# Layer 0's output in two passes over the chunks, and layer 1 placed ahead of the branch on the flag

## The chip, the cores and the metric

The kernel runs on one core of a Trainium2 chip. The metric is the device time of one execution in microseconds (us). Three runs of the kernel before took 7120.3, 7141.34 and 7145.82 us (median 7141.34). One further execution was recorded by the hardware profiler; it took 7152.27 us, of which 7150.5 us lie between its first and its last instruction (its span). All positions below, such as "at 6925.4", are us from the start of that span.

The engines are TensorE (PE; its weight loads are PEld), VectorE (DVE), ScalarE (ACT), GpSimd (POOL) and SyncE (SP). A row of SP or POOL with "q" is the issue of a DMA, not its transfer.

## The reference

Two layers work on 2708 nodes of 128 features, with a sparse adjacency matrix `adj` of 2708 x 2708. Layer 0 is a graph attention with 8 heads' worth of channels, layer 1 two graph convolutions. Each is followed by a residual sum and a normalisation over the features.

```python
# layer 0
q = (x @ Wq.T).reshape(d, n, h); k = ...; v = ...
a = einsum('dnh,dmh->dnm', q, k) * d ** -0.5 + adj + adj
out = einsum('dnm,dmh->dnh', softmax(a, axis=2), v)
x = layernorm(x + out.reshape(n, h * d) @ Wo.T)
# layer 1
local_hidden = adj @ (x @ W2) + b2
local_cross = adj @ (local_hidden @ W4) + b4
x = layernorm(x + local_cross + local_hidden @ res_w.T + res_b)
```

## The kernel before, in words

The kernel works in four stages. Everything is float32.

1. **Projections** (up to about 250 us): q, k and v are computed and written to HBM.
2. **Attention** (up to 6765): for 32 groups of 4 channels and 6 blocks of query nodes, scores, exponentials and their products with v. It leaves its sums in HBM as `os`: 8 rows of numerators and one row of denominators, for each channel and node. Its last result is copied out of PSUM at 6764.4 (line 377) and stored by four DMAs (line 379).
3. **Layer 0's output** (`layer0_out`, lines 479 to 516, up to 6915.8): the 2708 rows are worked on as 22 chunks (`MC`: 21 of 128 rows, one of 20). Each chunk goes through one long chain:
   - SP loads `ot` (128 x 9 x 128, 576 KB, in pieces of 512 bytes, line 484) and `xt` (64 KB, line 486).
   - DVE takes the reciprocal of the denominators (`rd`, line 488) and multiplies (`on`, line 490).
   - PE transposes `on` in 8 pieces into PSUM (`pt`, line 493), ACT copies that to SBUF (`oT`, line 495), and PE multiplies by Wo in 8 products (`py`, line 498; a float32 product is two matmul records in the profile).
   - DVE adds the residual (`y`, line 500) and takes the statistics (`st`, `mv`, lines 470 and 472), ACT takes the root (`sd`, 474), DVE inverts it (`rs`, 476) and normalises (`x1`, 477).
   - PE transposes `x1` (`px`, 511), ACT copies it (`x1T`, 513), PE multiplies by W2 (`pw`, 515), ACT copies the result (`xw`, 516).

   In the same loop DVE judges the result (`judge`): whether each denominator lies between two limits (`ok`, lines 503 to 505) and whether `y` is finite (lines 507 and 508), five instructions for each chunk. At the end the verdicts are brought down to one number, `n_fine` (lines 526 to 536).
4. **The branch and layer 1.** All engines load `n_fine` into a register (line 537) and branch (line 539). Where the verdict is bad, a slower attention (`attention_with_maxima`) and `layer0_out` are done again; with these inputs they are jumped over. Then layer 1 runs: for each of its two products, over 6 blocks of columns (`NBS`: 5 of 512, one of 148), `propagate` loads 22 tiles of `adjT` (256 KB each, `col`, issued by POOL at line 558, into 24 buffers) and PE multiplies each by the chunk of `xw` or `hw` that belongs to it, all into one accumulator (`acc`, line 559). After a block of the first product PE also multiplies by W4 (`ph`, 570); after a block of the second, by the residual weights (line 562), and the block's 4 row chunks are normalised and stored (line 584, issued by SP).

What sets the order: each engine works through its own instructions in order, and so do the DMA queues of SP and POOL: a DMA that waits holds all those behind it. Outside the attention, a scheduler chose that order when the program was built. In the order that it made, the chain of chunk c + 1 on PE stands behind that of chunk c at several places: `px` and `pw` of a chunk come ahead of the `py` of the next.

Pools set how far loads run ahead: three buffers for `ot` and `xt`, two for the accumulators in PSUM, 24 for `col`.

Of the kernel before, what the change touches and what calls it, by code (L numbers as in the profile page):

```python
# [9 lines left out]
F32 = mybir.dt.float32  # L10
F32R = mybir.dt.float32r
I32 = mybir.dt.int32
AF = mybir.ActivationFunctionType
ALU = mybir.AluOpType
AX = mybir.AxisListType
PSUM = bass.MemoryType.PSUM
DRAM = bass.MemoryType.DRAM

P = 128
H = 8  # L20
GB = 4
NB = 512
# [4 lines left out]
SUM_LOW = 1e-6  # L27
SUM_HIGH = 1e30


QK_LIMIT = 7.5
# [3 lines left out]
def chunks(n, w):  # L35
    return [(i, min(w, n - i)) for i in range(0, n, w)]
# [93 lines left out]
def graph_attention_gcn(ctx: ExitStack, tc: tile.TileContext, x, xT, adj, adjT, adjP, adjS,  # L130
# [325 lines left out]
        nc.sync.dma_start(t, src)  # L456
    nc.vector.tensor_add(bias, b4_sb, rb_sb)

    x1 = keep.tile([P, NM, D], F32, name="x1")
    xw = keep.tile([P, NM, D], F32, name="xw")  # L460
    hw = keep.tile([P, NM, D], F32, name="hw")
    lhT = keep.tile([P, N], F32, name="lhT")
    eps = keep.tile([P, 1], F32, name="eps")
    nc.vector.memset(eps, EPS)
    fine = keep.tile([P, NM + 1, 4], F32, name="fine")
    nc.vector.memset(fine, 1.0)

    def layernorm(to, y, w):
        st = stat.tile([P, nc.vector.BN_STATS_DIM], F32, tag="st", name="st")
        nc.vector.bn_stats(st[:w], y)  # L470
        mv = stat.tile([P, nc.vector.BN_AGGR_DIM], F32, tag="mv", name="mv")
        nc.vector.bn_aggr(mv[:w], st[:w])  # L472
        sd = stat.tile([P, 1], F32, tag="sd", name="sd")
        nc.scalar.activation(sd[:w], mv[:w, 1:2], AF.Sqrt, bias=eps[:w])  # L474
        rs = stat.tile([P, 1], F32, tag="rs", name="rs")
        nc.vector.reciprocal(rs[:w], sd[:w])  # L476
        nc.vector.tensor_scalar(to, y, mv[:w, 0:1], rs[:w], ALU.subtract, ALU.mult)  # L477

    def layer0_out(sb, ps, pa, judge):

        o3 = os_.rearrange("e (i g) -> i e g", g=P)
        for c, (i0, w) in enumerate(MC):
            ot = sb.tile([P, H + 1, P], F32, tag="ot", name="ot")
            nc.sync.dma_start(ot[:w], o3[ds(i0, w)])
            xt = sb.tile([P, D], F32, tag="xt", name="xt")
            nc.sync.dma_start(xt[:w], x[ds(i0, w), :])
            rd = sb.tile([P, P], F32, tag="rd", name="rd")
            nc.vector.reciprocal(rd[:w], ot[:w, H, :])
            on = sb.tile([P, H, P], F32, tag="on", name="on")
            nc.vector.tensor_mul(on[:w], ot[:w, :H, :], rd[:w].unsqueeze(1).to_broadcast([w, H, P]))  # L490
            pt = ps.tile([P, H, P], F32, tag="wide", name="pt")
            for e in range(H):
                nc.tensor.transpose(pt[:, e, :w], on[:w, e, :], ident[:w, :w])
            oT = sb.tile([P, H, P], F32, tag="oT", name="oT")
            nc.scalar.copy(oT[:, :, :w], pt[:, :, :w])
            py = pa.tile([P, NB], F32, tag="narrow", name="py")
            for e in range(H):
                nc.tensor.matmul(py[:w, :D], oT[:, e, :w], wo[:, e, :], start=(e == 0), stop=(e == H - 1))
            y = sb.tile([P, D], F32, tag="y", name="y")
            nc.vector.tensor_add(y[:w], py[:w, :D], xt[:w])  # L500
            if judge:
                ok = sb.tile([P, P], F32, tag="ok", name="ok")
                nc.vector.tensor_scalar(ok[:w], ot[:w, H, :], SUM_LOW, None, ALU.is_ge)
                nc.vector.scalar_tensor_tensor(ok[:w], ot[:w, H, :], SUM_HIGH, ok[:w], ALU.is_le, ALU.mult)
                nc.vector.tensor_reduce(fine[:w, c, 0:1], ok[:w], AX.X, ALU.min)
                finite = sb.tile([P, P], F32, tag="finite", name="finite")
                nc.vector.tensor_scalar(finite[:w], y[:w], 0.0, 0.0, ALU.mult, ALU.is_equal)
                nc.vector.tensor_reduce(fine[:w, c, 1:2], finite[:w], AX.X, ALU.min)
            layernorm(x1[:w, c, :], y[:w], w)
            px = pa.tile([P, NB], F32, tag="narrow", name="px")  # L510
            nc.tensor.transpose(px[:, :w], x1[:w, c, :], ident[:w, :w])
            x1T = sb.tile([P, P], F32, tag="x1T", name="x1T")
            nc.scalar.copy(x1T[:, :w], px[:, :w])
            pw = pa.tile([P, NB], F32, tag="narrow", name="pw")
            nc.tensor.matmul(pw[:w, :D], x1T[:, :w], w2, start=True, stop=True)
            nc.scalar.copy(xw[:w, c, :], pw[:w, :D])

    with ExitStack() as s:
        sb = s.enter_context(tc.tile_pool(name="sb1", bufs=3))
        ps = s.enter_context(tc.tile_pool(name="ps1", bufs=2, space=PSUM))  # L520
        pa = s.enter_context(tc.tile_pool(name="psa", bufs=2, space=PSUM))
        layer0_out(sb, ps, pa, True)
        for i in range(2):
            for j, (way, op) in enumerate(((ALU.max, ALU.is_le), (ALU.min, ALU.is_ge))):
                end = keep.tile([P, 1], F32, name=f"end{i}{j}")
                nc.vector.tensor_reduce(end, ends[:, i, j, :], AX.X, way)
                limit = QK_LIMIT * (1.0, half_scale)[i] * (1 if j == 0 else -1)
                nc.vector.tensor_scalar(fine[:, NM, 2 * i + j : 2 * i + j + 1], end, limit, None, op)
        every = keep.tile([P, 1], F32, name="every")
        nc.vector.tensor_reduce(every, fine.rearrange("p c t -> p (c t)"), AX.X, ALU.min)  # L530
        ones = keep.tile([P, 1], F32, name="ones")
        nc.vector.memset(ones, 1.0)
        pf = pa.tile([P, NB], F32, tag="narrow", name="pf")
        nc.tensor.matmul(pf[:1, :1], every, ones, start=True, stop=True)
        n_fine = keep.tile([1, 1], I32, name="n_fine")
        nc.vector.tensor_copy(n_fine, pf[:1, :1])
    rows_fine = nc.values_load(n_fine, min_val=0, max_val=P)

    with tc.If(rows_fine < P), ExitStack() as s:  # L539
        with ExitStack() as t:  # L540
            attention_with_maxima(t, tc, qs, ks, vs, os_, adj, adjT, ident)
        sb = s.enter_context(tc.tile_pool(name="sb0", bufs=2))
        ps = s.enter_context(tc.tile_pool(name="ps0", bufs=2, space=PSUM))
        pa = s.enter_context(tc.tile_pool(name="pa0", bufs=2, space=PSUM))
        layer0_out(sb, ps, pa, False)


    sb = ctx.enter_context(tc.tile_pool(name="sb2", bufs=3))
    cols = ctx.enter_context(tc.tile_pool(name="cols1", bufs=24))
    ps = ctx.enter_context(tc.tile_pool(name="ps2", bufs=2, space=PSUM))  # L550
    pa = ctx.enter_context(tc.tile_pool(name="pa2", bufs=2, space=PSUM))

    def propagate(src, n0, nw, last=None):

        acc = ps.tile([P, NB], F32, tag="wide", name="acc1")
        for m, (m0, mw) in enumerate(MC):
            t = cols.tile([P, NB], F32, tag="col", name="col1")
            nc.gpsimd.dma_start(t[:mw, :nw], adjT[ds(m0, mw), ds(n0, nw)])  # L558
            nc.tensor.matmul(acc[:, :nw], src[:mw, m, :], t[:mw, :nw], start=(m == 0),  # L559
                             stop=(last is None and m == NM - 1))  # L560
        if last is not None:
            nc.tensor.matmul(acc[:, :nw], *last, start=False, stop=True)  # L562
        return acc

    for n0, nw in NBS:
        acc = propagate(xw, n0, nw)
        nc.vector.tensor_scalar(lhT[:, ds(n0, nw)], acc[:, :nw], b2_sb, None, ALU.add)
        for i, w in chunks(nw, P):
            ph = pa.tile([P, NB], F32, tag="narrow", name="ph")
            nc.tensor.matmul(ph[:w, :D], lhT[:, ds(n0 + i, w)], w4, start=True, stop=True)  # L570
            nc.scalar.copy(hw[:w, (n0 + i) // P, :], ph[:w, :D])  # L571

    for n0, nw in NBS:
        acc = propagate(hw, n0, nw, (rw, lhT[:, ds(n0, nw)]))
        eT = sb.tile([P, NB], F32, tag="eT", name="eT")
        nc.vector.tensor_scalar(eT[:, :nw], acc[:, :nw], bias, None, ALU.add)  # L576
        for i, w in chunks(nw, P):
            pe = pa.tile([P, NB], F32, tag="narrow", name="pe")
            nc.tensor.transpose(pe[:w, :D], eT[:, ds(i, w)], ident)  # L579
            y = sb.tile([P, D], F32, tag="y", name="y1")  # L580
            nc.vector.tensor_add(y[:w], pe[:w, :D], x1[:w, (n0 + i) // P, :])  # L581
            o = sb.tile([P, D], F32, tag="xo", name="xo")
            layernorm(o[:w], y[:w], w)
            nc.sync.dma_start(out[ds(n0 + i, w), :], o[:w])


def attention_with_maxima(ctx, tc, qs, ks, vs, os_, adj, adjT, ident):
# [124 lines left out]
```

## Time and profile before

| | |
|---|---|
| runs | 7120.3, 7141.34, 7145.82 us |
| profiled execution, its span | 7152.27 us, 7150.5 us |
| PE, DVE, ACT, POOL busy in the span | 6813.9, 6156.5, 6560.1, 5755.0 us |
| attention's last copy ends | 6765.0 |
| layer 0's output: first reciprocal to the flag | 6767.5 to 6915.8 |
| branch, first load of layer 1 and first product | 6916.4, 6921.9, 6925.4 |
| layer 1: first product to the last normalised row | 6925.4 to 7148.0 |
| layer 0's output, one chunk: `rd`, `on` on DVE | 0.95, 1.21 us |
| `pt` (8 transposes) at full and half clock | 1.09, 1.97 us |
| `oT` on ACT | 1.01 us |
| `py` (16 records) at full and half clock | 1.95, 3.62 us |
| `y`, `st`, `mv` on DVE | 0.29, 0.28, 0.17 us |
| copy of 128 columns on ACT (`x1T`, `xw`) | 0.27 us |
| load of ACT's function table | 1.28 us |
| layer 1: one product, 128 x 512 (two records), full clock | 0.86 us |

How to read it: the busy shares of the page are averages over 7150 us, of which the attention is more than nine tenths, so they say nothing of the stages that the change touches. These are read by windows of time and by the timeline, whose rows give the start and the length of a group of instructions, the engine, the line, the operation, and in brackets how long the engine stood idle before it and what ended that. "PEclk" is the TensorE clock that was granted, as a share of full speed.

### The profile page before, as it was taken

What the parts mean: (1) busy time and instruction counts of PE and PEld (TensorE: products, weight loads), DVE (VectorE), ACT (ScalarE), POOL (GpSimd) and SP (SyncE); (2) the same over time, 40 slices, a digit from 0 to 9 for tenths busy, and PEclk for the clock granted to TensorE, in tenths of its full rate; (3) what the DMA queues carried; (4) which work ended last, traced back from release to release, by engine and by line L of the source; (5) the groups of instructions that cost most, each with busy time, mean ns of one, the idle gap of its engine ahead of it and who ended that gap; (6) DMA issues with size and microseconds to landing.
All of it is one profiled execution on the core that took longest, in us unless ns stands there. A gap on an engine that the chain in (4) does not pass through costs nothing. (4 is left out here: it accounts for less than half of the span.)

```text
span 7150.5 us, 136834 instructions
## 1 busy us (share of the span) xinstructions
PE 6813.9 (95%) x50426; PEld 2184.1 (31%) x50426; DVE 6156.5 (86%) x6292; ACT 6560.1 (92%) x3710; POOL 5755.0 (80%) x2525
## 2 busy tenths in 40 slices
PE   6599999999999999999999999999999999999979
PEld 2122233223332332222222332332322232323354
DVE  7589899989998998898899998998989998989831
ACT  3699999999999999999999999999999999999810
POOL 0578888888888888888888888888888888888625
PEclk9799999999999999999999999999999999999979
DMA  9776767767766767776677677677667767766647
GB/s 288 223 245 231 231 224 242 234 221 241 232 226 228 244 222 226 235 239 220 219 239 232 224 242 235 221 237 232 223 222 242 234 222 232 245 222 222 202 151 238
DMA packets 1101142, 1642.67 MB, mean 230 GB/s; under 512 B 144516, under 2 KB 1078804, under 8 KB 1096236
## 3 DMA queue, kind: packets, MB, share of 16 engines
q1 hardware_dynamic: 1081260, 1575.13, 67.7%
q0 software_dynamic: 19200, 58.68, 2.4%
q8 instruction: 399, 6.54, 0.4%
q14 instruction: 283, 2.32, 0.1%
HBM read 1551.44 MB, written 81.80 MB: 228 GB/s over the span
## 5 line engine op out<-in xcount | busy, mean ns | idle before, releaser
L441 POOL TENSOR_TENSOR w<-w,ecol 128x1356 f32<-128x1356 f32 (+1 forms) x1728 | 5351.6, 3104 | 925.2 <-ACT w L440 837.6
L357 DVE TENSOR_TENSOR e<-s,col 128x904 f32<-128x904 f32 (+1 forms) x4608 | 4830.4, 1092 | 483.9 <-PE s L350 172.7
L443 ACT ACTIVATE e<-e 128x2712 f32<-128x2712 f32 (+5 forms) x1728 | 4707.8, 2724 | 2.7 <-DVE e L357 2.5
L371 PE MATMUL acc<-e,vals 128*32 128x452 f32 x21888 | 3839.4, 557 | 11.4 <-ACT e L443 0.6
L350 PE MATMUL s<-q,k 32*128 32x452 f32 x10944 | 2464.1, 468 | 191.3 <-DVE e L357 80.6
L440 ACT ACTIVATE w<-p 128x1356 f32<-128x1356 f32 (+1 forms) x1728 | 2396.3, 1387 | 72.2 <-PE p L350 64.4
L350 PEld LDWEIGHTS s<-q,k 32*128 32x128 f32 x10944 | 1025.7, 182 | 3358.0 <-DVE e L357 2833.3
L371 PE MATMUL acc<-w,vals 128*32 128x452 f32 x10368 | 1670.2, 558 | 0.0
L350 PE MATMUL p<-q,k 32*128 32x452 f32 (+1 forms) x5184 | 1272.7, 439 | 12.3 <-ACT w L440 12.1
L357 DVE TENSOR_TENSOR e<-s,two 128x904 f32<-128x904 f32 (+1 forms) x960 | 1048.2, 1092 | 191.0 <-ACT w L440 82.6
L371 PEld LDWEIGHTS acc<-e,vals 128*32 128x32 f32 x21888 | 621.2, 108 | 855.0 <-issue 787.5
L350 PEld LDWEIGHTS p<-q,k 32*128 32x128 f32 x5184 | 521.2, 183 | 30.7 <-ACT w L440 30.1
L371 PEld LDWEIGHTS acc<-w,vals 128*32 128x32 f32 x10368 | 280.2, 108 | 205.1 <-issue 179.6
L558 POOL DMA_DIRECT2D col<-in_adjT x264 | 141.3, 537 | 231.9 <-SPq L539 159.2
L291 POOL CAST k<-k_raw 128x336 fp32r<-128x336 f32 x256 | 226.3, 886 | 15.1 <-DMA v_short<-vs 15.1
L367 PE MATMUL acc<-e,v_short 128*128 128x452 f32 (+1 forms) x384 | 196.7, 594 | 0.0
L233 POOL MEMSET k_short<- 128x128 f32 x2 | 0.3, 205 | 203.4 <-DMA vs<-po 203.4
L205 ACT ACTIVATE pr<-pp 128x1024 fp32r<-128x1024 f32 (+1 forms) x44 | 45.0, 1024 | 112.4 <-DMA ks<-pr 52.5
L377 DVE COPY o<-acc 128x452 f32<-128x452 f32 x192 | 118.5, 617 | 6.2 <-PE acc L371 6.2
L474 ACT ACTIVATE sd<-mv,eps 128x1 f32<-128x1 f32 (+1 forms) x44 | 12.5, 293 | 120.5 <-DVE mv L472 118.4
L559 PE MATMUL acc<-col,xw 128*128 128x512 f32 (+2 forms) x264 | 106.3, 556 | 9.8 <-DMA col<-in_adjT 9.8
L571 ACT COPY hw<-ph 128x128 f32<-128x128 f32 (+1 forms) x22 | 5.4, 266 | 115.3 <-PE ph L570 115.3
(73 smaller groups left out, 1251.0 us busy)
## 6 DMA issues: line engine op xcount, KB each, us to landing
col<-in_adjP SPq DMA_DIRECT2D x1965, 226.0 KB
two<-in_adjP SPq DMA_DIRECT2D x1440, 226.0 KB
ecol<-ne SPq DMA_DIRECT2D x1395, 226.0 KB
col<-in_adjP SPq DMA_DIRECT2D x393, 224.0 KB
two<-in_adjP SPq DMA_DIRECT2D x288, 224.0 KB
ecol<-ne SPq DMA_DIRECT2D x279, 224.0 KB
col<-in_adjT POOLq DMA_DIRECT2D x210, 256.0 KB, 4.5
k_raw<-ks SPq DMA_DIRECT2D x512, 84.6 KB
```

Source lines behind the costliest of these rows:

```text
L205: nc.scalar.mul(o[:mi, 0], flat, f)
L291: nc.gpsimd.tensor_copy(k[:, :, ts(i, n)], t[:, ts(i, n * NU)].rearrange("p (q c) -> p c q", c=NU))
L350: nc.tensor.matmul(to[:, :nw], k[r, m, :], q[r, :nw], start=True, stop=True)
L357: nc.vector.tensor_add(e[:, ds(at, 2), :nw], st[:, :, :nw], a)
L367: nc.tensor.matmul(a[:, :nw], vz, e[:, t, :nw], start=False, stop=False)
L371: nc.tensor.matmul(a[ds(32 * j, VW), :nw], v[:, m, ds(VW * j, VW)], e[:, t, :nw], start=(m == first_chunk), stop=(m == last_chunk))
L377: nc.vector.tensor_copy(o[:, :nw], acc.pop((g, b))[:, :nw])
L440: nc.scalar.activation(w[:, :, :nw], sp[:, :, :nw], AF.Exp, scale=2.0)
L441: nc.gpsimd.tensor_mul(w[:, :, :nw], w[:, :, :nw], exp_cols[g, b, two][:, :nw].unsqueeze(1).to_broadcast([P, 3, nw]))
L443: nc.scalar.activation(e[:, :at, :nw], e[:, :at, :nw], AF.Exp, scale=2.0)
L558: nc.gpsimd.dma_start(t[:mw, :nw], adjT[ds(m0, mw), ds(n0, nw)])
L559: nc.tensor.matmul(acc[:, :nw], src[:mw, m, :], t[:mw, :nw], start=(m == 0), stop=(last is None and m == NM - 1))
```

## The change

`layer0_out` is rewritten as passes over all chunks. The first is a loop with a pipeline written out by hand: `load` two chunks ahead, `divide` (load to `oT`) for chunk c, `project` (`py`) for chunk c - 1, `add_x` (`y` and its statistics) for chunk c - 2. The sums `y` of all chunks are kept in a new array `ys`, their means and variances in `mvs`. Behind the loop stand one root and one reciprocal for all 22 chunks, and a second pass in groups of four chunks: normalise, transpose into one PSUM tile `px`, one copy, multiply by W2 into one tile `pw`, one copy. The judging keeps, for each chunk, only the smallest and the largest denominator (`reach`); whether `ys` is finite is asked once for the whole array, after the second pass.

The order of these instructions is the written one (`manual_schedule`), engine by engine; layer 1's are still placed by the scheduler, which may put them between.

Layer 1 becomes a function. It is called right behind `layer0_out`, ahead of the branch, and its pool of 24 `col` buffers is opened before `layer0_out`'s pools. Its `col` loads are issued by SP and no longer by POOL. The branch comes last; its body does the slower attention and then both layers again (`rest(False)`).

```diff
+    nc.gpsimd.memset(eps, EPS)
+    nc.gpsimd.memset(ys[:, NM - 1, :], 0.0)
+    mvs = keep.tile([P, NM, nc.vector.BN_AGGR_DIM], F32, name="mvs")
+    nc.gpsimd.memset(mvs, 1.0)
...
-        for c, (i0, w) in enumerate(MC):
+        def load(c):
+            i0, w = MC[c]
             ot = sb.tile([P, H + 1, P], F32, tag="ot", name="ot")
             nc.sync.dma_start(ot[:w], o3[ds(i0, w)])
             xt = sb.tile([P, D], F32, tag="xt", name="xt")
             nc.sync.dma_start(xt[:w], x[ds(i0, w), :])
+            given[c] = ot, xt
+
+        def divide(c):
+            w, ot = MC[c][1], given[c][0]
             rd = sb.tile([P, P], F32, tag="rd", name="rd")
             nc.vector.reciprocal(rd[:w], ot[:w, H, :])
+            if judge:
+                for i, op in enumerate((ALU.min, ALU.max)):
+                    nc.vector.tensor_reduce(reach[:w, i, c : c + 1], ot[:w, H, :], AX.X, op)
             on = sb.tile([P, H, P], F32, tag="on", name="on")
...
+        def project(c):
+            w, oT = MC[c][1], turned.pop(c)
+            made[c] = pa.tile([P, NB], F32, tag="py", name="py", bufs=2)
...
+        def add_x(c):
+            w = MC[c][1]
+            nc.vector.tensor_add(ys[:w, c, :], made.pop(c)[:w, :D], given.pop(c)[1][:w])
+            statistics(mvs[:w, c, :], ys[:w, c, :], w)
...
-                ok = sb.tile([P, P], F32, tag="ok", name="ok")
-                nc.vector.tensor_scalar(ok[:w], ot[:w, H, :], SUM_LOW, None, ALU.is_ge)
-                nc.vector.scalar_tensor_tensor(ok[:w], ot[:w, H, :], SUM_HIGH, ok[:w], ALU.is_le, ALU.mult)
-                nc.vector.tensor_reduce(fine[:w, c, 0:1], ok[:w], AX.X, ALU.min)
-                finite = sb.tile([P, P], F32, tag="finite", name="finite")
-                nc.vector.tensor_scalar(finite[:w], y[:w], 0.0, 0.0, ALU.mult, ALU.is_equal)
-                nc.vector.tensor_reduce(fine[:w, c, 1:2], finite[:w], AX.X, ALU.min)
-            layernorm(x1[:w, c, :], y[:w], w)
-            px = pa.tile([P, NB], F32, tag="narrow", name="px")
-            nc.tensor.transpose(px[:, :w], x1[:w, c, :], ident[:w, :w])
-            x1T = sb.tile([P, P], F32, tag="x1T", name="x1T")
-            nc.scalar.copy(x1T[:, :w], px[:, :w])
-            pw = pa.tile([P, NB], F32, tag="narrow", name="pw")
-            nc.tensor.matmul(pw[:w, :D], x1T[:, :w], w2, start=True, stop=True)
-            nc.scalar.copy(xw[:w, c, :], pw[:w, :D])
...
+        load(0)
+        load(1)
+        for c in range(NM + 2):
+            if c + 2 < NM:
+                load(c + 2)
+            if c < NM:
+                divide(c)
+            if 0 <= c - 1 < NM:
+                project(c - 1)
+            if c >= 2:
+                add_x(c - 2)
+        sd, rs = (sb.tile([P, NM], F32, tag=n, name=n) for n in ("sds", "rss"))
+        nc.scalar.activation(sd, mvs[:, :, 1], AF.Sqrt, bias=eps)
+        nc.vector.reciprocal(rs, sd)
+        for c0 in range(0, NM, 4):
...
+            for c in cs:
+                w = MC[c][1]
+                nc.vector.tensor_scalar(x1[:w, c, :], ys[:w, c, :], mvs[:w, c, 0:1], rs[:w, c : c + 1],
+                                        ALU.subtract, ALU.mult)
+                nc.tensor.transpose(px[:, c - c0, :w], x1[:w, c, :], ident[:w, :w])
+
+            full = len([c for c in cs if MC[c][1] == P])
+            parts = [(0, full, P)] + [(c - c0, 1, MC[c][1]) for c in cs if MC[c][1] < P]
+            for i, n, w in parts:
+                nc.scalar.copy(x1T[:, ds(i, n), :w], px[:, ds(i, n), :w])
+            for c in cs:
+                w = MC[c][1]
+                nc.tensor.matmul(pw[:w, c - c0, :], x1T[:, c - c0, :w], w2, start=True, stop=True)
+            for i, n, w in parts:
+                nc.scalar.copy(xw[:w, ds(c0 + i, n), :], pw[:w, ds(i, n), :])
+        if judge:
+            finite = sb.tile([P, NM * D], F32, tag="finite", name="finite", bufs=1)
+            nc.vector.tensor_scalar(finite, ys.rearrange("p c f -> p (c f)"), 0.0, 0.0, ALU.mult, ALU.is_equal)
+            nc.vector.tensor_reduce(fine[:, 0:1], finite, AX.X, ALU.min)
...
+            nc.tensor.matmul(pf[:1, :1], every, ones, start=True, stop=True)
+            nc.vector.tensor_copy(n_fine, pf[:1, :1])
...
-            nc.gpsimd.dma_start(t[:mw, :nw], adjT[ds(m0, mw), ds(n0, nw)])
+                nc.sync.dma_start(t[:mw, :nw], adjT[ds(m0, mw), ds(n0, nw)])
...
+    def rest(judge):
+        with ExitStack() as s:
+            cols = s.enter_context(tc.tile_pool(name="cols1", bufs=24))
+            with ExitStack() as t:
+                sb = t.enter_context(tc.tile_pool(name="sb1", bufs=3))
+                ps = t.enter_context(tc.tile_pool(name="ps1", bufs=2, space=PSUM))
+                pa = t.enter_context(tc.tile_pool(name="psa", bufs=1, space=PSUM))
+                t.enter_context(tc.manual_schedule())
+                layer0_out(sb, ps, pa, judge)
+            layer1(s, cols)
+
+    n_fine = keep.tile([1, 1], I32, name="n_fine")
+    rest(True)
     rows_fine = nc.values_load(n_fine, min_val=0, max_val=P)
-    with tc.If(rows_fine < P), ExitStack() as s:
+    with tc.If(rows_fine < P):
         with ExitStack() as t:
             attention_with_maxima(t, tc, qs, ks, vs, os_, adj, adjT, ident)
-        layer0_out(sb, ps, pa, False)
+        rest(False)
```

The order of the changed program's instructions, engine by engine, is known before it runs. On SP the four stores of `os` and the loads of the weights come first, then three pairs of `ot` and `xt`; from there a pair stands as "xt of chunk c, then ot of chunk c + 1", with one or two `col` loads behind it, until 24 `col` tiles are placed. `xt` of chunk c waits for `add_x` of chunk c - 3, because it takes over that chunk's buffer. Behind the 29th `col` load stands its load of `n_fine` into a register. On PE the products of layer 1's first block stand one by one between the groups of the second pass (five of them), and the product `pf` that sums the verdicts stands ahead of the sixth.

## The prediction

> **What bounds the kernel now.** The chain of waits that ended last lies wholly in layer 1 and is PE's (line 559), so ahead of 6921 it tells nothing. I read the tail by windows of time first; columns: length, busy time of PE, PEld, DVE, ACT, POOL with counts, granted clock, DMA share, GB/s.
>
> ```profile
> 6841.00:6878.00 37.00, 24.92 (x193) 21.93 (x191) 22.05 (x71) 13.87 (x30) 0.00 (x0) 1.00 0.13 38
> 6878.00:6913.00 35.00, 24.11 (x103) 19.99 (x103) 6.80 (x31) 5.43 (x17) 0.00 (x0) 0.51 0.02 5
> 6913.00:6926.00 13.00, 1.21 (x6) 0.92 (x7) 1.52 (x8) 0.73 (x3) 4.13 (x8) 0.63 0.24 69
> 6936.00:7140.00 204.00, 204.00 (x553) 94.07 (x552) 23.67 (x95) 9.64 (x38) 129.41 (x242) 1.00 0.82 271
> ```
>
> In layer 1 (last row) PE is never idle: it is the bound there. In layer 0's output (first two) no engine is full, DMA is idle: a chain of latencies. Around the branch (third) nothing works. The timeline shows the chain for one chunk at full clock, and for one of the last five at half clock:
>
> ```profile
> 6866.90 1.01 ACT L495 COPY oT<-pt 128x1024 f32<-128x1024 f32 x1 [1.58 <-PE py L498]
> 6867.96 1.09 PE L493 MATMUL pt<-ident,on 128*128 128x128 f32 x8 [1.16 <-ACT oT L495]
> 6869.90 1.95 PE L498 MATMUL py<-wo,oT 128*128 128x128 f32 x16
> 6871.94 1.01 ACT L495 COPY oT<-pt 128x1024 f32<-128x1024 f32 x1 [1.57 <-PE py L498]
> ...
> 6891.19 0.29 DVE L500 TENSOR_TENSOR y<-py,xt 128x128 f32<-128x128 f32 x1 [5.20 <-PE py L498]
> ```
>
> A chunk takes 5.04 us at full clock (6866.90 to 6871.94): ACT copies only once `py` is done, PE transposes only once ACT has copied. The last five take 7.1 each. The waits of SP, and two reciprocals with the loads they wait for:
>
> ```profile
> SPq L486 <- DVE finite L507: 80.6, 19, 7.0
> SPq L539 <- SPq L539: 4.1, 1, 4.1
> ```
>
> ```profile
> 6821.32 0.37 SPq L484 DMA_DIRECT2D ot<-os  x1
> ...
> 6825.12 4.03 SPq L484 DMA_DIRECT2D ot<-os  x2
> ...
> 6826.20 0.95 DVE L488 RECIPROCAL rd<-ot 128x128 f32<-128x128 f32 x1 [0.42 <-DMA ot<-os]
> ...
> 6829.62 0.95 DVE L488 RECIPROCAL rd<-ot 128x128 f32<-128x128 f32 x1 [0.34 <-DMA ot<-os]
> ```
>
> SP waits 80 us in all for DVE to free an `xt` (a wait for several at once; line 500 is the reader). The other pair: from the issue of an `ot` to its use pass 4.9 us (the 17th, 6821.32 to 6826.20) and 4.5 us (the 18th, 6825.12 to 6829.62). The branch takes 4.1 us.
>
> I call E the moment when PE starts the sixth product of layer 1, since the new order puts five of them into the second pass. Before: first product 6925.4; at half clock a record takes 0.86 us to about 6930.2, then 0.43: ten records end at **E = 6932.0**. Behind E the work is the same.
>
> **First pass.** Up to the first `ot` SP's list is nearly the old one (four stores, weights, biases); the old trace has its next load at 6771.28, where `ot` of chunk 0 now stands (two were loaded before the attention's end, so this start is later than now). Plus 4.7 us of landing: first reciprocal 6776.0, 8.5 us later than now. From first reciprocal to first `y` the trace has 9.95 us (6767.52 to 6777.47, half clock); two reductions of 0.25 come in between: **first `y` at 6786.4**.
>
> From then on each engine's share of a chunk is: PE 1.09 + 1.95 = 3.04; ACT 1.01; DVE 0.95 + 2 x 0.25 + 1.21 + 0.29 + 0.28 + 0.17 = 3.40 by durations, about 3.2 by starts, since instructions overlap by some 0.06 (`on` follows `rd` at 0.87). The new order takes ACT and PE off each other's back. What is late next is **SP**: `ot` of chunk c + 1 stands behind `xt` of chunk c, and that waits for `add_x` of c - 3. From the end of one `y`: `xt` and `ot` issue 0.4, landing 4.7, `rd` 0.87, two reductions 0.4, `on` 1.2, `y` 0.3 = 7.9 us to the `y` two chunks on, so **3.9 us a chunk**. The `col` loads share the DMAs: 24 tiles, 1 or 2 a chunk; at 369 GB/s (10 us window from 6926) one takes 0.7 us, and part of that stands ahead of an `ot`; I add 0.1 us over 13 chunks: 3.95 on average. The DMAs carry 640 + 384 KB a chunk: 2.8 us at that rate, 3.9 at the 267 GB/s of the best slice of layer 0's output, so they may just share the bound. 19 chunks x 3.95 = 75 us: 6861.4; the last two `y` come without loads, 0.5 + 2.5 + 0.67 + 0.3 + 1.95 + hops = 6.7: **last `y` at 6868.1**.
>
> The clock: here the Trainium skill speaks against the change. "TensorE: Matmul & The Clock Gate", Part 4, says that transposes do not count as work that raises the clock. Without them PE would be busy 1.95 / 3.95 = 49% of a chunk; in the first window (full clock) the products are (14.23 + 3.42) / 37 = 48%, in the second (half clock) (18.09 + 3.99) / 35 = 63%, doubled by the slow clock. So products alone don't tell the two windows apart, and I go by the first row: 67% busy with transposes held full clock for 37 us, and the new loop has 3.04 / 3.95 = 77%. By the rule PE could stay at half clock: 1.97 + 3.62 = 5.6 us a chunk, PE the bound, 19 x 1.65 = 31 us later.
>
> **Second pass.** Now 22 chains of `st` to `xw` stand in the loop; they become: statistics 0.45, the table load 1.28 (it stands behind the wait for the last `mv`, so it is paid here), root 0.29, reciprocal 0.16, first four `x1` about 1.2, `px` 0.5 to 0.9, hops: 5 us. Then six groups, each a copy 128 x 512 (0.59, between 0.27 for 128 columns and 1.01 for 1024), `pw` (8 records, 1.0 at full and 1.8 at half clock), another copy 0.59, hops 0.4: 2.6 us by ACT; by PE `px`, `pw` and one product of layer 1, 2.3 at full, 4.4 at half clock. I take 2.8 x 5.5 = 15.5: `pf` is due at 6888.6. DVE meanwhile: 22 `x1` (0.26 apart) to 6876, then `finite` over 2816 columns (0.225 for 128; by 1.0 to 1.4 ns a column from the 512-wide rows: 3 to 4), its reduction 3, twelve small ones 2.5: 6885 to 6887. Hidden, just. If it were 3 us late, PE would stand at `pf`. **E = 6888.6, 43.4 us earlier.** I give back 1 us for a window at half clock behind it.
>
> **Judging** in the loop falls from 1.25 to 0.5 us of DVE a chunk; worth nothing by itself, DVE was not the bound.
>
> **Layer 1.** PE stays the bound. `col` issues move from POOL (0.54 each) to SP (0.35 to 0.43), one per 0.86 us of PE: covered by 24 buffers. Behind SP's load of `n_fine` wait `col` loads from the 30th on, until about 6888; 24 tiles lie ready, 20 us of PE. Each `out` store now stands ahead of `col` loads; the worst waits some 9 us (from the 16th product of a block to its end and 3 us of normalising), with loads for 12 us in hand. Bounds: 0 to 3 us in all; I take 0. The memsets on POOL are hidden, POOL has been idle since 6762.7.
>
> **The end.** The branch's gap (n_fine at 6915.8 to the first product 6925.4) is in the 43.4. It comes back once behind the last store: 4.1 us of branch and 0.6 of semaphore resets, in place of the 1.1 us in which SP now awaits the store's landing: **+3.6**. If fetching the code ran ahead: +0; if both branches of the end miss: +7.7.
>
> **Sum:** -43.4 + 1 + 3.6 = **-38.8 us**. Against the profiled execution 7152.27: 7113.5. The runs' median is 11 us lower than that, and I take the difference from it: 7141.3 - 38.8 = **7102 us**. The attention's instructions and their order are unchanged.
>
> **Rivals.**
> - *DVE sets the loop*: `ot` lands earlier, as the three buffers suggest, 3.2 us a chunk: 19 x 0.75 = 14 us better, 7088. For: DVE's durations alone. Against: the order of `xt` and `ot` on SP. 20%.
> - *Half clock* through the loop, as worked out: 7133; partial windows, 7120. For: ahead of 6841 the clock flipped all the time. Against: a PE that is full at half clock was raised again (6838 to 6841). 16%.
> - *Slower*: `col` loads ahead of `ot` on SP's queue hold it up. Price: 0.5 us a chunk for each us of landing, 19 chunks. The gain of 39 is gone at 4.1 us more, 8.8 us of landing; at 10 us: 7102 + 19 x 2.65 = 7152. For: five `col` loads stand in one row behind the fourth `ot`. Against: only 1 or 2 a chunk follow, and DMA was 13% busy. 4%.
> - *It doesn't do what it says*: the scheduler could leave layer 1 behind the flag. The order shows the opposite; none.
>
> The likeliest, SP's loop, has the remaining 60%, by itself 7092 to 7114.
>
> **Numbers.** A measurement tells about 0.5% (36 us) from nothing: the line is at 7105.6. Of the likeliest case 70% lies below it: 42 + 20 = 62% faster, 18 + 16 = 34% the same, 4% slower. The range 7078 to 7128 leaves out the far ends of the first two rivals and the third.
>
> **What will show it.** `rd` about 3.9 us apart and waiting for `ot`; if for PE, half clock. Clock 1.0 from about 6790 on. `pf` near 6888. PE without idle time behind it. Some 4 us between the last store and the end. Wrong would be: `rd` at 3.2 or over 5 us apart, or PE waiting for `col`.

## The result and the profile after

The changed kernel takes 7108.9 us (median of 8 runs, 7088.4 to 7116.2) against 7145.8 us of the kernel before (8 runs): a ratio of 0.995, 95% interval 0.9934 to 0.9966, so between 24 and 47 us off. The profiled execution spans 7109.3 us where the one of before spans 7150.5. The attention is unchanged, but its end differs from one execution to the next (6765.0 us in the first, 6772.3 in the second), so from here on each stage is counted from the end of the attention's last copy, and **tail** is what comes behind that copy.

| us behind the attention's last copy | before | after |
|---|---|---|
| first reciprocal `rd` | 2.5 | 9.5 |
| first `y` added | 12.2 | 18.1 |
| last `y` added | 147.7 | 95.8 |
| sixth product of layer 1 (E) | 167.1 | 115.1 |
| last `xo` | 383.0 | 331.1 |
| end of the span | 385.5 | 337.0 |
| at half clock, up to the last `xo` | 81.9 | 21.4 |

The positions in the table are starts; that of the last `xo` is its end. First the windows of the changed kernel (columns as before): the loop, the start of the second pass, layer 1, and what follows the last `xo`.

```profile
6791.00:6863.00 72.00, 52.90 (x449) 50.00 (x448) 57.48 (x132) 19.23 (x19) 0.00 (x0) 1.00 0.75 223
6869.00:6877.00 8.00, 4.92 (x17) 3.76 (x18) 6.28 (x24) 3.35 (x5) 0.00 (x0) 0.59 0.00 1
6888.00:7091.00 203.00, 203.00 (x540) 92.83 (x538) 22.07 (x90) 9.68 (x38) 0.00 (x0) 1.00 0.81 260
7103.42:7109.30 5.88, 0.00 (x0) 0.00 (x0) 0.01 (x1) 0.00 (x0) 0.00 (x0) 0.50 0.09 24
```

The loop runs at full clock throughout, and still no engine is full in it: PE 73%, DVE 80%, the DMA engines 75%. Something else sets its pace. Layer 1 is PE's to the last microsecond, as it was. The last row is the new end: 5.9 us in which nothing computes. The timeline shows two chunks of the loop:

```profile
6817.60 0.28 DVE L521 TENSOR_TENSOR ys<-py,xt 128x128 f32<-128x128 f32 x1
...
6817.91 0.33 SPq L495 DMA_DIRECT2D xt<-in_x  x1
...
6818.28 0.43 SPq L493 DMA_DIRECT2D ot<-os  x1
...
6819.07 0.95 DVE L501 RECIPROCAL rd<-ot 128x128 f32<-128x128 f32 x1 [0.64 <-DMA ot<-os]
...
6823.03 0.95 DVE L501 RECIPROCAL rd<-ot 128x128 f32<-128x128 f32 x1 [0.80 <-DMA ot<-os]
...
6825.36 0.28 DVE L521 TENSOR_TENSOR ys<-py,xt 128x128 f32<-128x128 f32 x1
```

Read it as a circle. The addition into `ys` at 6817.60 frees an `xt`; only then SP issues the waiting `xt` load (6817.91) and behind it the `ot` load (6818.28); 4.75 us later the reciprocal that needs this `ot` starts (6823.03, DVE had idled for it), and its iteration ends with the next addition but one, 6825.36. That is 7.76 us for two chunks. The waits of SP say the same, and price the branch:

```profile
SPq L495 <- DVE st L473: 51.0, 19, 4.2
...
SPq L630 <- SPq L630: 2.9, 1, 2.9
```

All 19 `xt` loads that need a used buffer wait, 51 us together. (DVE's line is that of the instruction nearest to the event; the reader of `xt` is the addition just ahead of it.) The branch itself is 2.9 us at the end; before, it was 4.1 us in the middle. The second pass, in the timelines of ACT, DVE and PE:

```profile
6869.04 1.28 ACT L536 ACT_TABLE_LOAD   x1 [4.36 <-DVE mvs L474]
...
6883.04 0.16 DVE L571 TENSOR_REDUCE every<-fine 128x1 f32<-128x7 f32 x1
...
6887.32 0.19 PE L574 MATMUL pf<-ones,every 128*1 128x1 f32 x2
6887.45 7.99 PE L588 MATMUL acc<-col,xw 128*128 128x512 f32 x18
```

The table load stands on the path behind the last statistics. The flag's chain on DVE is done at 6883.2, and PE comes to `pf` only at 6887.3: the chain is hidden, with 4 us to spare. The sixth product starts at 6887.45. (Here and below, a row of layer 1's products is cut where the view ends: its 7.99 us and x18 are not the whole group.)

### The profile page after: what moved, and what is told of

Read it like the earlier page. It is cut to its first block, busy times and chain, and to the rows that moved or that the text cites. A ratio compares the mean times of both kernels' runs of the same rounds, so it can differ in the third digit from the quotient of the medians.

```text
span 7109.3 us, 136670 instructions
## 1 busy us (share of the span) xinstructions
PE 6795.0 (96%) x50426; PEld 2165.0 (30%) x50426; DVE 6148.8 (86%) x6208; ACT 6549.0 (92%) x3659; POOL 5613.7 (79%) x2266
## 3 DMA queue, kind: packets, MB, share of 16 engines
q1 hardware_dynamic: 1117908, 1633.81, 70.8%
## 4 chain that ended last, share of the span: by engine, by line
PE 45%; DMA 16%; ACT 11%; DVE 8%; POOL 8%; issue 8%; SPq 3%; DVEq 0%; ACTq 0%; POOLq 0%
PE acc L371 22%; PE s L350 15%; POOL w L441 8%; DVE e L357 7%; ACT e L443 6%; DMA col<-in_adjP 6%; ACT w L440 4%; DMA ecol<-ne 4%; PE acc L588 3%; DMA k_raw<-ks 2%; DMA two<-in_adjP 2%; PE p L350 2%; PE acc L367 2%; SPq L315 1%; DMA ks<-pr 1%
## 5 line engine op out<-in xcount | busy, mean ns | idle before, releaser
L588 PE MATMUL acc<-col,hw 128*128 128x512 f32 (+2 forms) x264 | 104.1, 545 | 0.0
L210 DVE TENSOR_REDUCE ends<-pr 128x1 f32<-128x1024 f32 (+1 forms) x88 | 102.7, 1207 | 0.0
```

What stands on the lines that cost most here:

```text
L210: nc.vector.tensor_reduce(ends[:mi, int(dst is qs), i, c : c + 1], o[:mi, 0].bitcast(F32), AX.X, op)
```

## The experiments

### SP's order taken out of the loop

```diff
-            xt = sb.tile([P, D], F32, tag="xt", name="xt")
+            xt = sb.tile([P, D], F32, tag="xt", name="xt", bufs=6)
```

> The changed kernel with six xt buffers in place of three, so that SP no longer stops at an xt load with the next ot load behind it. If SP's order sets the loop (my step), ot arrives in time and DVE sets it: reciprocals 3.2 to 3.4 us apart in place of 3.9, first y to last y about 68 us in place of 77.7, and the whole 8 to 12 us faster than the changed kernel. If instead the loads' landing or the DMA engines' rate sets the loop (1 MB a chunk with its col loads), the spacing stays at 3.8 to 3.9 us and the time is the changed kernel's within 2 us.

Measured: first to last `y` 63.3 us against 77.7; tail 323.5 against 337.0; 7089.3 us (5 runs), ratio to before 0.9927 (0.9913 to 0.9942). The window of its loop, SP's waits on the loads, and PE's waits in that window:

```profile
6776.00:6836.00 60.00, 55.14 (x469) 52.02 (x468) 57.37 (x134) 19.52 (x20) 0.00 (x0) 1.00 0.92 268
```

```profile
SPq L493 <- DVE ys L521: 28.1, 16, 2.7
...
PE pt L509 <- DVE on L506: 4.9, 19, 0.7
```

The waits at the `xt` line (L495) are gone; DVE is now 96% busy, PE 92%. In the window's 60 us PE waits 19 times for DVE's `on` (the last row), while DVE waits for nothing. A chunk takes 3.0 us, even less than the 3.2 I had for DVE. So SP's order set the pace, and neither the landing of the loads nor the DMA engines' rate did: they carry the same bytes 14 us faster, at 92% busy. With the cause removed, the "DVE sets the loop" rival of the prediction comes true, and at its price: 14 us there, 13.5 us of the tail here. (That the times agree too, 7088 there and 7089 here, is in part luck.)

### The two halves of the change, one at a time

The passes alone (the branch back between layer 0 and layer 1; the `col` loads stay on SP):

```diff
-    rest(True)
+    part0(True)
     rows_fine = nc.values_load(n_fine, min_val=0, max_val=P)
     with tc.If(rows_fine < P):
...
-        rest(False)
+        part0(False)
+    with ExitStack() as s:
+        cols = s.enter_context(tc.tile_pool(name="cols1", bufs=24))
+        layer1(s, cols)
```

> The passes alone: layer 0 as in the changed kernel, then the flag's branch where it was, then layer 1. By my steps the loop is as fast as in the changed kernel; behind it the branch's gap (about 9.7 us from n_fine to the first product) and ten records partly at half clock come back, some 14 us, against 3.4 us less at the end and some 6 us less at the start (ot stands ahead of the weights on SP again): about 4 us slower than the changed kernel, 33 to 45 us faster than before. If the order of layer 1 and branch carried the gain, it would be 15 us or more slower than the changed kernel.

Measured: tail 350.9 us, 353.3 in a second profile; 7121.7 us (14 runs), ratio 0.9966 (0.9951 to 0.998). That is 14 to 16 us behind the changed kernel's tail, not 4; it reaches the 15 us of the alternative, so the order carries more of the gain than I gave it. DVE and PE at the start of its layer 0, then PE at the end, from the timelines:

```profile
6789.01 0.95 DVE L501 RECIPROCAL rd<-ot 128x128 f32<-128x128 f32 x1 [3.35 <-DMA os<-o]
...
6795.70 0.95 DVE L501 RECIPROCAL rd<-ot 128x128 f32<-128x128 f32 x1 [3.23 <-DMA ot<-os]
6798.04 0.94 DVE L501 RECIPROCAL rd<-ot 128x128 f32<-128x128 f32 x1
6798.17 1.97 PE L509 MATMUL pt<-ident,on 128*128 128x128 f32 x8 [4.70 <-DVE on L506]
...
6799.94 3.54 PE L517 MATMUL py<-wo,oT 128*128 128x128 f32 x16
...
6803.51 0.29 DVE L521 TENSOR_TENSOR ys<-py,xt 128x128 f32<-128x128 f32 x1 [3.07 <-PE py L517]
...
6902.53 0.24 PE L574 MATMUL pf<-ones,every 128*1 128x1 f32 x2
6911.55 13.98 PE L588 MATMUL acc<-col,xw 128*128 128x512 f32 x27 [8.78 <-DMA col<-in_adjT]
```

Two things I had wrong. Its first reciprocal is 6 us earlier (SP takes one `ot` ahead of the weights again), and nothing comes of it: the second waits for an `ot` that stands behind the weights, and on PE the first `py` stands behind the second chunk's transposes (6798.17, at half clock), so the first addition waits 3.07 us for it. And the second pass without products of layer 1 in it stays at half clock: 34.1 us of the stretch to the sixth product in both profiles, against 6.8 in the changed kernel. The windows, first from the first `px` to `pf` in the passes alone, then in the changed kernel up to the moment when its clock is back:

```profile
6882.02:6902.77 20.75, 16.85 (x68) 13.81 (x68) 11.53 (x36) 6.10 (x12) 0.00 (x0) 0.50 0.00 0
...
6873.80:6877.20 3.40, 3.40 (x14) 2.66 (x14) 3.40 (x13) 1.17 (x2) 0.00 (x0) 0.50 0.00 0
```

In the passes alone PE is 81% busy there, and the clock stays at half for all 20.75 us; in the changed kernel the first product of layer 1 (6876.08) closes the gap in front of the next `pw`, PE is busy without a break, and the clock is full from 6877.2. The stretch from the last `y` to the sixth product is 39.3 us instead of 19.3. Of these 20 us, 8.8 are PE's wait around the branch, 6.5 the five products, which now stand behind it, and about 4.6 the pass itself, which takes 23.8 us to `pf` instead of 19.1 although it has less to do.

The order alone (layer 0 by chunk as before, layer 1 ahead of the branch, `col` loads on SP):

```diff
     def layer0_out(sb, ps, pa, judge):
...
-        load(0)
-        load(1)
-        for c in range(NM + 2):
+        for c, (i0, w) in enumerate(MC):
...
-                t.enter_context(tc.manual_schedule())
                 layer0_out(sb, ps, pa, judge)
             layer1(s, cols)
```

> The order alone: layer 0's output chunk by chunk as before, layer 1 ahead of the branch, col loads on SP. By my steps the chain stays at 5.0 us a chunk at full clock and 7.1 at half, last y some 135 us behind the first; only the gap of the branch goes (about 16 us from n_fine to the sixth product) and 3.4 us come at the end: 10 to 16 us faster than before, 25 to 30 us slower than the changed kernel. If products of layer 1 that now fit into the chain's gaps kept the clock up, the last five chunks would take 5 us and it would be up to 25 us faster than before.

Measured: tail 359.9 us and 360.1 in a second profile; 7110.2 us (6 runs, 7086 to 7142), ratio 0.9945 (0.9927 to 0.9963). PE in the last chunks:

```profile
6910.50 1.95 PE L505 MATMUL py<-wo,oT 128*128 128x128 f32 x16
6912.28 2.74 PE L551 MATMUL acc<-col,xw 128*128 128x512 f32 x6
...
6914.97 1.02 PE L551 MATMUL acc<-col,xw 128*128 128x512 f32 x2
...
6916.05 1.95 PE L505 MATMUL py<-wo,oT 128*128 128x128 f32 x16
```

The alternative came nearer than my steps: in the gaps of the last three chunks stand three or four products of layer 1 each. A chunk there takes 5.6 us instead of 7.1, with up to 3.4 us of layer 1 done inside it, at full clock. The chain as a whole, first to last `y`, takes 130.6 and 129.6 us with 29 and 31 us of it at half clock; before, it is 135.5 us with 61, or 130.4 with 44 in the second profile below. So the chain itself is hardly shorter: the gain is the products that are already done at its end, and the gap around the branch.

### Both kernels profiled a second time

> The kernel before, profiled a second time. Its tail behind the attention's end (385.5 us in the first profile, 95 us of it at half clock or in flips) tells whether the profiled gain of the tail, 48.5 us, against 37 us between the medians is the attention's scatter or the old tail's own: if the old tail is steady, it is 385 within 2 us again and only the attention's end moves (6765 us, within 25); if its clock flips differ, the tail is shorter, 375 or so.

> The changed kernel, profiled a second time. With no half clock in its loop the tail has little to vary by: 337 us within 2; the attention's end moves freely (6772 us in the first profile, within 25).

Measured: before, attention's end 6785.4, tail 378.5; after, 6753.6 and 337.2. So the changed tail is steady, the old one is not: with 61.4 us at half clock instead of 81.9 it was 7 us shorter. What the change is worth behind the attention is then 41 to 48 us (378.5 or 385.5 less 337), the passes alone 25 to 35, the order alone 18 to 26. Added up the halves give 43 to 61, so they share some of it; which part they share is not shown.

Over all 13 profiles here the attention ended between 6752.2 and 6785.7 us (standard deviation 11.3), and late where it had been long at half clock (171 to 218 us of it; correlation 0.89). This scatter lies on every measured time. It can account for the six runs of the order alone that come out level with the changed kernel, whose tail is 23 us shorter. The mean clock of each run tells its time at half clock (twice the missing share of the span): 206 us on average in those six runs, 224 in the eight of the changed kernel, although the tail of the order alone holds some 17 us more of it. So their attention had about 35 us less, which is worth 19 to 27 us by an estimate from the two pairs of profiles (20.4 us for 37.6 us of half clock before, 18.7 for 23.9 in the changed kernel). The same working on the runs of the kernel before (247 us, 63 to 84 of it in the tail) goes the way of the medians, which show 37 us where the tails show 41 to 48.

### The branch taken out

```diff
-    rows_fine = nc.values_load(n_fine, min_val=0, max_val=P)
-    with tc.If(rows_fine < P):
-        with ExitStack() as t:
-            attention_with_maxima(t, tc, qs, ks, vs, os_, adj, adjT, ident)
-        rest(False)
```

> The changed kernel without the branch and what it guards (the repeat of attention and both layers is left out). If the branch costs at the end what I took, the stretch from the last xo to the end of the span falls from 5.9 to about 2.5 us, and nothing ahead of it moves. If the branch instead cost something inside layer 1 (n_fine's load on SP), a wait of SP behind it would go too, and the stretch from the sixth product to the last xo, 216.0 us, would shrink.

Measured: from the last `xo` to the end 2.25 us instead of 5.9; from the sixth product to the last `xo` 216.0 us as before, as in the changed kernel. The branch costs 3.6 us at the end and nothing inside layer 1. Ahead of it something did move: the sixth product comes 2.2 us later than in the changed kernel, in a loop that has 3.4 us at half clock here and none there.

### Do transposes hold the clock?

```diff
             for e in range(H):
-                nc.tensor.matmul(made[c][:w, :D], oT[:, e, :w], wo[:, e, :], start=(e == 0), stop=(e == H - 1))
+            extra = pa.tile([P, 4, P], F32, tag="px", name="extra")
+            for e in range(2 * H - 2):
+                nc.tensor.transpose(extra[:w, e % 4, :], oT[:, e % H, :w], ident)
+            nc.tensor.matmul(made[c][:w, :D], oT[:, 0, :w], wo[:, 0, :], start=True, stop=True)
```

> The changed kernel with transposes in place of the loop's products: seven of the eight heads' products of y are left out, and fourteen more transposes a chunk, which nobody reads, stand there, so that PE is busy about as long with hardly any product. If transposes do not count for the clock (the rule), the loop runs at half clock: a transpose record 0.24 us instead of 0.13, granted clock 0.5 for the whole loop. If they count (my reading of the row of before), the clock stays at 1.0 from about 17 us behind the attention's end, as in the changed kernel.

Measured (this kernel leaves out seven of the eight heads' products of `y`), windows of the same 60 us of its loop, first all engines, then the products of the loop alone (PE, PEld, clock, DMA):

```profile
6796.00:6856.00 60.00, 43.65 (x371) 40.77 (x372) 47.43 (x109) 15.44 (x16) 0.00 (x0) 1.00 0.72 212
...
6796.00:6856.00 60.00, 5.80 (x30) 4.53 (x30) 1.00 0.72 212
```

PE is busy 73% of the time, with products 10%, and the granted clock is 1.00 for all 60 us (products take 50% of these positions in the changed kernel). Ahead of the window the clock had been at half once, for 3.4 us from 6789.0, after 3.4 us in which PE was busy 33%, and had come back. Transposes count, at least with a tenth of products among them. The rule of the Trainium skill ("TensorE: Matmul & The Clock Gate", Part 4) does not hold for these fp32 transposes, and the row was the better guide.

### A version that beats both

```diff
+        with tc.high_priority():
             load(0)
             load(1)
+            load(2)
...
             nc.scalar.copy(turned[c][:, :, :w], pt[:, :, :w])
+            if c == 0:
+                early = sb.tile([P, 1], F32, tag="early", name="early", bufs=1)
+                nc.scalar.activation(early, rd[:, :1], AF.Sqrt)
...
+            if c == 18:
+                roots(0, 16)
+            if 20 <= c:
+                weigh(c - 20)
+            if 19 <= c < 23:
+                turn(c - 19)
```

(With six `xt` buffers. `turn` and `weigh` are the two halves of a group of the second pass: `x1`, `px`, its copy; `pw`, its copy. The flag's product is moved behind layer 1's first block.)

> The changed kernel with four edits: six xt buffers; the first three ot and xt loads ahead of the weights on SP; the table of the root loaded behind the first copy instead of behind the last statistics; the second pass of chunks 0 to 15 put into the end of the loop, so that products of layer 1 cover the last root. From the stages of the runs so far: first y 3 to 6 us sooner after the attention's end (18.7 to about 13), loop 63 plus up to 5 us for what it takes in, last y to sixth product (20.1) 12 us shorter or more. Tail behind the attention 305 to 315 us against 323.5 with six xt buffers alone and 337.0 in the changed kernel; whole about 7075. If the loop is now PE's and DVE's together, what is moved into it costs there what it saves behind, and the tail stays above 318.

Measured: 7069.8 us (6 runs), ratio 0.9905 (0.9881 to 0.9929). First `y` at 13.7 us, first to last `y` 74.8, last `y` to the sixth product 8.8; tail 319.6. Against six `xt` buffers alone, the start and the second pass gain 5 and 11 us, and the loop gives the 11 back, so the alternative held: what is moved into the loop costs there what it saves behind. DVE's rows show part of where:

```profile
6769.68 0.95 DVE L501 RECIPROCAL rd<-ot 128x128 f32<-128x128 f32 x1 [2.93 <-DMA ot<-os]
...
6823.40 0.25 DVE L535 RECIPROCAL rss<-sds 128x16 f32<-128x16 f32 x1 [1.73 <-ACT sds L534]
...
6844.90 0.19 DVE L535 RECIPROCAL rss<-sds 128x6 f32<-128x6 f32 x1 [3.43 <-ACT sds L534]
```

The first two stand in the loop, the third behind its last `y`. The loop also has 5.4 us of waits for `py` in four places and 16 of the `x1`, 0.26 us each.

The same with these three waits attacked (the small weights behind the sixth `ot`, `wo` behind the second, each root issued earlier on ACT):

> The version with four edits, mended where its trace shows waits: the small weights behind the sixth ot load on SP instead of ahead of the fourth (reciprocal of the fourth waited 2.9 us for ot), wo between the second and third ot, the first root issued ahead of chunk 18's copy on ACT (DVE waited 1.7 us for it), the second root ahead of the third group's copy (DVE waited 3.4 us). If these waits are on the path, 4 to 8 us come off: tail 312 to 316 us against 319.6. If PE and DVE are full there anyway, the waits move and the tail stays within 2 us.

Measured: loop 70.8, tail 316.2; 7082.3 us (6 runs, 7048.7 to 7086.6), ratio 0.9906 (0.9881 to 0.9931). The profile shows 3.4 us of the 4 to 8; the times, with the attention's scatter on them, can't tell the two versions apart. Either is about 0.9% faster than the kernel before. Most of what they have over the changed kernel comes from the six `xt` buffers (tail 323.5 us); what the other edits add shows in the tails, 4 and 7 us, and not clearly in the times (ratio 0.9927 with the buffers alone).

## Why the prediction was right, step by step

- **The bound of the loop** was right in mechanism: `rd` waits for `ot`, `ot` stands behind a waiting `xt`. Taking the wait out took 14 us. The term was a little large: first to last `y` 81.7 us predicted, 77.7 and 78.1 measured (3.7 us a chunk). Two chunks take the 7.8 us of the sum in mid-loop; the first and last are quicker. The 0.1 us for the `col` loads, 1.3 us in all, is neither shown nor excluded: without them the loop took 75.3 and 77.7.
- **The start**: first `rd` 7.0 us later than before (8.5 predicted). First `y` only 5.9 later instead of 8.9: from `rd` to the end of `y` it took 8.9 us, not the 9.95 of the old trace plus two reductions, for a good part because the first `py` ran at full clock (1.98 us; 3.20 in the old trace). The step was also built on the wrong instruction: the passes alone showed that the second chunk's load, whose transposes stand ahead of the first `py` on PE, decides on the first `y`, and not the first chunk's.
- **The clock**: full from 16.1 us behind the attention's end, and in the loop no half clock. The prediction's 6790 was 25 us behind it, in the old trace's positions; that the positions agree (6788.5) is chance.
- **Second pass**: 20.5 us from last `y` to E predicted, 19.3 measured. DVE's chain came out shorter (`finite` 1.6 us, not 3 to 4) and ended 4 us ahead of need. What I hadn't seen is how much depends on layer 1's products in it: they bring the clock back, and without them the pass up to `pf` takes 4.6 us longer.
- **Layer 1**: 216.0 us from E to the last `xo`, 215.9 before; SP's merged queue costs nothing, and neither was the microsecond for half clock needed.
- **The end**: +3.4 us measured between the profiles, 3.6 predicted.
- **The sum**: E came 52.0 us earlier in the tail, not 43.4 (some 3.0 from the start, 4.0 from the loop, 1.2 from the second pass), so the tail shrank by 48.5 in the profiled pair where I had 38.8. The old tail of that profile was a long one; with the second profile it is 41.3. The medians' 37 us are nearer to the 38.8 than the profiles are. That is in part luck: steps that were too large by some 8 us, and the attention's scatter the other way. The slower rival, `ot` held up by `col` loads, never showed: from the fifth on an `ot` was used 4.3 to 5.5 us after its issue, far from the 8.8 at which the gain would have been gone. The fourth, with five `col` loads behind it, was used after 6.9 us, and DVE did not wait for it.
- **The chance**: the line between faster and the same was put at 0.5%, with 62% for faster. The ratio, 0.995 (0.9934 to 0.9966), lies on that line. That the change saves time is clear; that it passes the line is not.

Left open: what makes the attention of the same kernel differ by up to 20 us between executions. It goes with its time at half clock. Each fall to half clock in it follows 3.4 us in which PE was busy less than 75%, and such stretches mostly lie about 200 us, or a multiple of it, apart, near the borders of its 32 groups (about 203 us each, an estimate from 6500 us). Why the clock falls at a border in one execution and not in the next, no run here shows.

## What to carry to other kernels

When a loop has no full engine and its loads share one queue, look for a load that stands behind another load's wait for a buffer: a few more buffers of the small tile were worth 14 us here. Independent matrix work put into the gaps of a chain of latencies pays twice, by its own time and by the clock that it keeps up. Where a stage is moved ahead of a branch, count the branch at its new place too, and compare by the tail behind the last unchanged stage when that stage scatters more than the change is worth.

## What the hardware showed that was not expected

- Transposes in fp32 hold the clock as products do: 73% of PE's time, 10% of it products, at clock 1.00 for 60 us.
- A second pass that kept PE 81% busy at half clock (16.85 of 20.75 us) did not bring the clock back; with layer 1's products in it, 3.4 us with PE busy throughout did. The changes of the clock in all 13 profiles lie on a grid of 3.41 us. Cut along it, all 348 falls to half clock follow a step with PE busy less than 75%, and all 335 returns a step with PE busy at least 78%; of the steps at half clock with at least 80%, 334 of 513 were followed by full clock.
- The same program's attention takes 6754 or 6772 us (the changed kernel), 6765 or 6785 us (before), with 24 and 38 us more at half clock in the longer one.
